# Masking the keys of a decoder's cross attention before they are spread over even and odd heads

## The chip, the cores and the metric

The kernel runs on one core of one Trainium2 chip. Its time is the device time of one launch in microseconds (us), and less is better. Times of several launches are given as a median with the lowest and the highest.

## What is computed

Sixteen independent samples of 128 tokens and 256 features pass through a two-layer decoder in float32. Layer 0 has a causal attention over 16 heads with rotary positions, a linear cross attention and a gated feed-forward part whose operands are rounded to a 4-bit grid. Layer 1 has a causal attention with two score products, a softmax cross attention with a feed-forward part of 1024 hidden features, and a last product whose operands are rounded to a 6-bit grid. A layer normalisation stands after each of the six parts. The change lies in the softmax cross attention of layer 1, of which this is the core:

```python
Q = _split_heads(x @ Wq + bq)          # 16 heads of 16
K = _split_heads(y @ Wk + bk)
V = _split_heads(y @ Wv + bv)
scores = jnp.einsum('bhqd,bhkd->bhqk', Q, K) * scale
scores = jnp.where(mask == 0, jnp.float32(-1000000000.0), scores)
probs = jax.nn.softmax(scores, axis=-1)
attn = jnp.einsum('bhqk,bhkd->bhqd', probs, V)
```

`y` is the context and `mask` has one whole number for each of the 128 context tokens. The kernel sets a masked key to zero (it multiplies the keys by `mb`, which is 0 or 1) and adds the large negative number in the score product through a further small matmul with `mr`.

## The kernel before

**Work of one sample.** The function `stages(b, s)` runs sample `b` in place `s`, one of `NS = 8` sets of buffers, through `l0_attn`, `l0_xattn`, `l0_ffn`, `l1_attn`, `l1_xattn` and `l1_ffn`. Each of these is a generator. Between two `yield`s stands a step: the instructions of mostly one engine. A `yield` names the engine of the next step and what this needs: tiles that must be written, and places in shared rings such as `"p"` (four PSUM banks for products), `"quad"` (the single score tile of four banks) or `"t2"`.

**The order of the work.** All engines stand under a manual schedule: each executes its instructions in the order in which they were recorded. The loop at the end of `decoder_kernel` writes this order when the program is built. It keeps a `Clock` with modelled costs of every instruction (`Timed._cost`), asks each live sample when its next step could begin (`Run.start`), and takes among the steps that could begin within 0.05 of the earliest one by a rank of readiness, age and a table `DELAY`. So the order depends on the modelled cost of each step, and one other cost or one further step can change the order of all later steps of all samples. The DMA issues of SyncE (context, mask, input, output) are recorded in the same order.

**Fillers.** Where the plan leaves TensorE idle for 1.4 us or more, `Timed.fill` records matmuls without use (`ps_filler`, line 161) for three quarters of the planned gap, at a price of 512 columns each. They keep TensorE active.

**The cross attention's keys.** `l1_xattn` (line 1106) loads the mask (`mi`), makes `mb` and `mr` on VectorE, and projects the context into the PSUM tile `ps_x1k`: 2 x 128 columns, two groups of dense features. The score product needs a head on 32 partitions of which half are zero, so `by_parity` (line 560) writes four groups of 128 columns to `k`, two with the even heads and two with the odd heads, by four ScalarE activations that multiply by a column of zeros and ones (`parity`) and add a bias that has been multiplied by the same column (columns 14 to 17 of `bc`). GpSimd then multiplies the 512 columns of `k` by `mb`, in place. The query tile `q` takes a buffer of the ring `B` of its place at the start of the function, and is written only after the query product.

**Names of the later steps.** In `l1_attn` the last product is `ps_op_a` (`out_proj`), with `ps_yt` ahead of it. In `l1_xattn` follow `ps_x1k`, `ps_x1v` (values), `ps_tr_x` (transposition of the sample's state, copied to `yT_x`), `ps_x1q` (query product), `ps_s_x` (scores, whose maxima `nm_x` VectorE takes), `ps_tm_x` (transposed maxima), `ps_st_x` (transposed scores, to `e_x` by the exponential), `ps_yp_x` (weighted values, copied to `ys_x`), `ps_ty_x`, `ps_tr_x1y`, `ps_op_x` (output product), `ps_tr_x1t`, and the feed-forward part: two halves of the first product and the second product, all called `ps_ff` in the profile. In `l1_ffn` VectorE rounds the state (`f1q`, with one step `fc_f` on ScalarE), and `ps_tr_f`, `ps_op_f` and the last layer normalisation lead to `out`.

Of the kernel before, what the change touches and what calls it, by code (L numbers as in the profile page):

```python
# [11 lines left out]
AF = mybir.ActivationFunctionType  # L12
ALU = mybir.AluOpType
AX = mybir.AxisListType

B, T, D, H, HD, LAT = 16, 128, 256, 16, 16, 32
P = 128
# [196 lines left out]
def decoder_kernel(ctx: ExitStack, tc: tile.TileContext, a: dict, out: bass.AP):  # L214
    nc = tc.nc
    clock = Clock()
    V, S, PE, GP = (
        Timed(clock, n, e) for n, e in (("V", nc.vector), ("S", nc.scalar), ("PE", nc.tensor), ("GP", nc.gpsimd))
    )
# [12 lines left out]
    def ring(pool, tag, bufs, shape, dtype, name):  # L232

        t = pool.tile(shape, dtype, tag=tag, name=name, bufs=bufs)
        held = rings.setdefault(tag, [])
        size[tag] = bufs
        opened.append(t)
        clock.kept.add(clock.key(t))
        if len(held) >= bufs:
            old = min(held, key=clock.ends)  # L240
            held.remove(old)
            clock.read[Clock.key(t)] = ("", clock.done(old))
        held.append(t)
        return t

    def mine(s, tag, shape, name, dtype=F32):

        return ring(own, f"{tag}{s}", 1, shape, dtype, name)
# [34 lines left out]
    def arrives(t):  # L283
        clock.wrote[clock.key(t)] = ("Q", max(clock.free["PE"], clock.free["Q"]) + 2.5)
# [53 lines left out]
    def row(name):  # L338
        at = ROW[name]
        return rows[:, at.start - NADD : at.stop - NADD]  # L340
# [55 lines left out]
    parity, parity_half = (const.tile([P, 2], F32, tag=n, name=n) for n in ("parity", "parity_half"))  # L396
# [41 lines left out]
    def bank(shape, name, dtype=F32):  # L438
        return psum(ps_p, "p", shape, name, dtype)

    def work(tag, bufs, shape, name, dtype=F32):
        return ring(wk, tag, bufs, shape, dtype, name)
# [29 lines left out]
    def bias_row(p, name):  # L472

        if name == "l2o":
            g, src = 0, bl
        else:
            g, c, n = place[name]
            src = bt[:, c : c + n]
        PE.matmul(p, lhsT=sel[:, g, :], rhs=src, start=True, stop=False)
# [15 lines left out]
    def layernorm(dst, h, name):  # L495
        m, r, mr = yield from moments(h, name)
        GP.tensor_scalar(mr, m, r, -1.0, ALU.mult, ALU.mult)
        yield "S", mr, h
        S.activation(dst, h, AF.Identity, bias=mr, scale=r)

    def layernorm_affine(dst, h, g, shift, name):

        m, r, _ = yield from moments(h, name)
        yield "V", m
        V.scalar_tensor_tensor(h, h, m, row(g), ALU.subtract, ALU.mult)
        yield "V", r, shift, h
        V.scalar_tensor_tensor(dst, h, r, shift, ALU.mult, ALU.add)
# [3 lines left out]
    def new_x(b, s, name):  # L511

        return mine(s, "x", [P, D], f"x_{name}_{b}")
# [10 lines left out]
    def project(p, weight, rhs):  # L524

        for c in range(p.shape[1]):
            for kc in range(2):
                PE.matmul(
                    p[:, c, :], lhsT=weight[:, kc, c * P : (c + 1) * P], rhs=rhs[:, kc, :], start=(kc == 0),
                    stop=(kc == 1),  # L530
                )

    def biased(dst, p, bias, func=AF.Identity, scale=1.0):

        for c in range(p.shape[1]):
            S.activation(dst[:, c, :], p[:, c, :], func, bias=bias[:, c : c + 1], scale=scale)

    def dense_col(name):
        at = 2 * [n for n, _, _ in DENSE].index(name)
        return bc[:, at : at + 2]  # L540

    def product(p, lhsT, weight, name):

        bias_row(p, name)
        n = lhsT.shape[1]
        for c in range(n):
            PE.matmul(p, lhsT=lhsT[:, c, :], rhs=weight[:, c, :], start=False, stop=(c == n - 1))
# [12 lines left out]
    def by_parity(dst, p, at):  # L560

        for o in range(2):
            biased(dst[:, 2 * o : 2 * o + 2, :], p, bc[:, at + 2 * o : at + 2 * o + 2], scale=parity[:, o : o + 1])
# [108 lines left out]
    def with_bias(b, s, name, tag):  # L672

        t = mine(s, tag, [P, D], f"xb_{name}_{b}")
        GP.tensor_tensor(t, xs[b], row(name), ALU.add)
        return t

    def features(y, s, at, name):

        yT = mine(s, at, [P, 2, P], f"yT_{name}")  # L680
        yield from transposed(y, 2, yT, name)
        return yT

    def out_proj(yT, weight, bias, residual, s, at, name):

        yield "PE", "p", yT
        p = bank((D,), f"op_{name}")
        product(p, yT, weight, bias)
        yield "V", p
        h = mine(s, at, [P, D], f"h_{name}")  # L690
        V.tensor_tensor(h, p, residual, ALU.add)
        return h
# [124 lines left out]
    def values(s, name):  # L817

        v = mine(s, "v", [P, H * VW + HD], f"v_{name}")
        GP.memset(v[:, H * VW :], 0.0)  # L820
        return v
# [284 lines left out]
    def l1_xattn(b, s, ctx_):  # L1106
        yield "V", "mi"
        mi = work("mi", 2, [P, P], f"mi_{b}", I32)
        nc.sync.dma_start(out=mi, in_=a["mask"][:, b * T : (b + 1) * T].partition_broadcast(P))
        q = mine(s, "B", [P, 2, P], f"x1q_{b}")  # L1110
        k = mine(s, "C", [P, 4, P], f"x1k_{b}")
        arrives(mi)
        yield "V", "mb", mi

        mb = work("mb", 2, [P, P], f"mb_{b}")
        V.tensor_scalar(mb, mi, 0.0, None, ALU.not_equal)
        mr = mine(s, "mr", [P, P], f"mr_{b}", BF16)
        V.tensor_scalar(mr, mi, 0.0, terms, ALU.is_equal, ALU.mult)
        yield "PE", "p", ctx_, mb
        p = bank((2, P), f"x1k_{b}")  # L1120
        project(p, w["w_x1k"], ctx_)
        yield "S", p, mb
        by_parity(k, p, 14)
        yield "GP", k, mb
        GP.tensor_tensor(k, k, mb.unsqueeze(1).to_broadcast([P, 4, P]), ALU.mult)
        yield "PE", "p", ctx_
        p = bank((H * VW,), f"x1v_{b}")
        product(p, ctx_, w["w_x1v"], "x1v")
        yield "S", p
        v = values(s, f"x1_{b}")  # L1130
        S.copy(v[:, : H * VW], p)
        xT = yield from features(xs[b], s, "A", f"x1_{b}")
        yield "PE", "p", xT
        p = bank((2, P), f"x1q_{b}")
        project(p, w["w_x1q"], xT)
        yield "S", p
        biased(q, p, dense_col("x1q"), scale=HD**-0.5)
        y = yield from attention(b, s, q, k, v, mr, f"x1_{b}", "A")
        yT = yield from features(y, s, "B", f"x1y_{b}")
        h = yield from out_proj(yT, w["w_x1o"], "x1o", xs[b], s, "D", f"x1_{b}")  # L1140
        t = mine(s, "C", [P, D], f"x1_{b}")
        yield from layernorm_affine(t, h, "g1", row("be1"), f"x1i_{b}")
        tT = yield from features(t, s, "B", f"x1t_{b}")
        ff = []
        for i in range(2):
            yield "PE", "p", tT
            p = bank((4, P), f"ff_{b}_{i}")
            project(p, w["w_1"][:, :, 4 * i * P : 4 * (i + 1) * P], tT)
            yield "S", p
            ff.append(mine(s, "AD"[i], [P, 4, P], f"ff{i}_{b}"))  # L1150
            biased(ff[i], p, cols[:, COL["b1"].start + 4 * i : COL["b1"].start + 4 * i + 4], AF.Relu)
        xb = with_bias(b, s, "be2", "B")
        yield "PE", "p", ff[0]
        p = bank((D,), f"ff2_{b}")
        bias_row(p, "x1b2")
        for c in range(8):
            if c == 4:
                yield "PE", ff[1], p
            PE.matmul(p, lhsT=ff[c // 4][:, c % 4, :], rhs=w["w_2"][:, c, :], start=False, stop=(c == 7))
        yield "V", p  # L1160
        h = mine(s, "A", [P, D], f"h_ff_{b}")
        V.tensor_tensor(h, p, t, ALU.add)
        z = mine(s, "C", [P, D], f"z_x1_{b}")
        yield from layernorm_affine(z, h, "g2", xb, f"x1j_{b}")
        xs[b] = new_x(b, s, "x1")
        yield from layernorm(xs[b], z, f"x1_{b}")
# [14 lines left out]
    def stages(b, s):  # L1181
        ctx_ = yield from l0_attn(b, s)
        yield from l0_xattn(b, s, ctx_)
        yield from l0_ffn(b, s)
        ctx_ = yield from l1_attn(b, s)
        yield from l1_xattn(b, s, ctx_)
        yield from l1_ffn(b, s)
        release(f"place{s}", [xs[b]])
# [214 lines left out]
```

## Time and profile before

| what | value |
|---|---|
| device time, median of three | 964.27 us (961.06 to 965.34) |
| device time of the profiled execution | 960.91 us |
| its span, first to last instruction | 959.2 us |
| TensorE matmuls busy | 891.0 us (93%) |
| TensorE weight loads busy | 711.3 us (74%) |
| VectorE busy | 701.0 us (73%) |
| ScalarE busy | 515.7 us (54%) |
| GpSimd busy | 432.5 us (45%) |
| DMA, mean | 27 GB/s |

The profile comes from one execution, whose own time is 1.71 us above its span and 3.36 us below the median. Busy times of different engines lie beside each other, so they don't add up. In the groups of instructions each row has an engine, an operation, the tile written and those read, the count, then the summed busy time and the mean in ns, and behind the second bar the idle time of the engine ahead of these instructions and what ended it. Nearly all rows have line 208, that of the recording helper, so they are told apart by tiles. Sample numbers are left out of tile names in the profile; they stand in the recorded order of the built program.

### The profile page before, as it was taken

The page shows a single profiled execution, that of the slowest core. Times are in us where ns is not written, and L with a number is a line of the kernel's source. Part 1 is how long each engine was busy: PE and PEld are TensorE (multiplying, and loading weights), DVE is VectorE, ACT ScalarE, POOL GpSimd, SP SyncE. Part 2 cuts the span into 40 slices and gives each one's busy share as a digit, 9 for nine tenths or more (in the row PEclk, how much of TensorE's full clock was granted, in tenths as well). Part 3 has the DMA queues.
Part 4 walks back from the last instruction along what each step waited for, and adds up shares of the span by engine and source line. Part 5 has one row for each costly group of instructions (what it writes and reads, how often), then busy time and mean ns, then how long its engine had stood idle before and what let it go on. Part 6 is the DMA issues. An engine that isn't in the chain of part 4 may idle for free.

```text
span 959.2 us, 28184 instructions
## 1 busy us (share of the span) xinstructions
PE 891.0 (93%) x11882; PEld 711.3 (74%) x11882; DVE 701.0 (73%) x1440; ACT 515.7 (54%) x1119; POOL 432.5 (45%) x898
## 2 busy tenths in 40 slices
PE   6788999899999999999999999998999999999985
PEld 6575666676878788878887776776777878877863
DVE  5899999778975945554768788759858687654564
ACT  3254374475577555555455456546765664654532
POOL 3325444465444446343444454554435353453332
PEclk9999999999999999999999999999999999999998
DMA  7920100000000000010000000000000000100000
GB/s 232 207 71 7 29 13 2 15 10 10 11 23 5 12 27 20 18 30 13 13 15 27 23 25 23 13 13 11 15 10 7 16 6 2 37 5 24 2 12 11
DMA packets 47863, 25.55 MB, mean 27 GB/s; under 512 B 23005, under 2 KB 45517, under 8 KB 47481
## 3 DMA queue, kind: packets, MB, share of 16 engines
q1 hardware_dynamic: 46816, 22.39, 8.6%
q8 instruction: 93, 1.52, 0.6%
q0 software_dynamic: 192, 0.93, 0.4%
q10 hardware_dynamic: 728, 0.44, 0.2%
q14 instruction: 34, 0.27, 0.1%
HBM read 19.57 MB, written 2.10 MB: 23 GB/s over the span
## 4 chain that ended last, share of the span: by engine, by line
PE 53%; DVE 30%; ACT 6%; POOL 6%; issue 4%; POOLq 0%; ACTq 0%; DVEq 0%
PE ps_ff L208 10%; PE ps_s_a L208 3%; DVE nm_a L208 3%; PE ps_st_a L208 3%; DVE rope L208 3%; PE ps_a1qk L208 2%; DVE hh L208 2%; PE ps_st_x L208 2%; PE ps_qk L208 2%; PE ps_dn L208 2%; PE ps_pg L208 2%; PE ps_yt L208 2%; PE ps_pu L208 2%; PE ps_yp_a L208 2%; PE ps_s_x L208 2%
## 5 line engine op out<-in xcount | busy, mean ns | idle before, releaser
L208 POOL TENSOR_SCALAR_AFFINE_SELECT e_a<-e_a 128x1024 f32<-128x1024 f32 x64 | 78.4, 1227 | 75.4 <-ACT e_a L208 75.2
L208 DVE TENSOR_REDUCE nm_a<-ps_s_a 128x16 f32<-128x2048 f32 x32 | 73.1, 2283 | 17.3 <-PE ps_s_a L208 17.2
L208 ACT ACTIVATE e_a<-ps_st_a 128x1024 f32<-128x1024 f32 x64 | 65.7, 1032 | 17.7 <-PE ps_st_a L208 17.5
L208 ACT ACT_TABLE_LOAD x47 | 60.3, 1283 | 12.7 <-DMA brow<-in_rows_dram 8.8
L208 PE MATMUL ps_ff<-yT_x1t,w 128*128 128x128 f32 x512 | 62.9, 276 | 0.5 <-ACT yT_x1t L208 0.5
L208 PEld LDWEIGHTS ps_ff<-yT_x1t,w 128*128 128x128 f32 x512 | 60.1, 192 | 2.4 <-issue 0.9
L208 PE MATMUL ps_ff<-w,ff 128*128 128x256 f32 x256 | 61.3, 383 | 0.0
L208 PEld LDWEIGHTS ps_ff<-w,ff 128*128 128x128 f32 x256 | 46.3, 190 | 7.6 <-issue 1.8
L208 ACT ACTIVATE ff<-ps_ff,cols 128x128 f32<-128x128 f32 x128 | 36.6, 370 | 27.4 <-PE ps_ff L208 27.0
L208 POOL CAST maxima<-nm_a 128x16 bf16<-128x16 f32 x32 | 9.8, 307 | 89.1 <-DVE nm_a L208 89.1
L208 PE MATMUL ps_dn<-qw_down,hT 128*128 128x256 f32 x192 | 47.5, 384 | 1.1 <-ACT yT_x1t L208 1.1
L208 DVE TENSOR_REDUCE nm_x<-ps_s_x 128x16 f32<-128x2048 f32 x16 | 36.5, 2282 | 11.4 <-PE ps_s_x L208 11.4
L208 PE MATMUL ps_pg<-gu,yT_xq 128*128 128x352 f32 x128 | 44.1, 467 | 0.1
L208 PE MATMUL ps_pu<-gu,yT_xq 128*128 128x352 f32 x128 | 43.1, 459 | 0.0
L208 ACT ACTIVATE x_x<-z_x,rstd_x 128x256 f32<-128x256 f32 x32 | 19.2, 601 | 42.5 <-POOL rstd_x L208 39.2
L208 PEld LDWEIGHTS ps_dn<-qw_down,hT 128*128 128x128 f32 x192 | 34.6, 190 | 8.0 <-issue 2.1
L208 ACT ACTIVATE e_x<-ps_st_x 128x1024 f32<-128x1024 f32 x32 | 31.5, 1023 | 15.7 <-PE ps_st_x L208 15.7
L208 ACT ACTIVATE x_a<-h_a,rstd_a 128x256 f32<-128x256 f32 x32 | 19.3, 603 | 31.8 <-POOL rstd_a L208 30.6
L208 PE MATMUL ps_yp_a<-e_a,v_a 128*32 128x128 f32 x1024 | 35.3, 276 | 1.1 <-POOL e_a L208 1.1
L208 POOL TENSOR_TENSOR rot<-rope,rope 128x512 f32<-128x512 f32 x16 | 21.3, 1330 | 29.6 <-DVE rope L208 27.8
L208 PEld LDWEIGHTS ps_pu<-gu,yT_xq 128*128 128x128 f32 x128 | 24.3, 190 | 13.5
L208 POOL TENSOR_TENSOR x1k<-x1k,mb 128x512 f32<-128x512 f32 x16 | 21.8, 1365 | 27.2 <-ACT x1k L208 27.2
(367 smaller groups left out, 2638.0 us busy)
## 6 DMA issues: line engine op xcount, KB each, us to landing
ctx<-in_ctxT_dram SPq DMA_DIRECT2D x32, 128.0 KB
xT_in<-in_xT_dram SPq DMA_DIRECT2D x16, 128.0 KB
w<-in_w_dram SPq DMA_DIRECT2D x2, 1024.0 KB
x_in<-in_x_dram SPq DMA_DIRECT2D x16, 128.0 KB
out_dram<-out SPq DMA_DIRECT2D x16, 128.0 KB
a1qa<-x_f SPq DMA_DIRECT2D x16, 127.0 KB
mi<-in_mask_dram SPq DMA_DIRECT2D x16, 64.0 KB
rows<-in_rows_dram POOLq DMA_DIRECT2D x1, 768.0 KB, 5.7
```

Of the source, the lines that this page charges most:

```text
L208: return f(*args, **kw)
```

## The change

The projection is no longer spread and then masked. Two activations write the dense keys with their bias to a new tile `kb` of 2 x 128 columns, GpSimd multiplies these 256 columns by `mb` in place, and two further activations of 256 columns each write them to `k`, multiplied by the column of even heads and by that of odd heads. A step of ScalarE after GpSimd's is new. `kb` lives in the ring `B`, so `q` is taken from this ring later, just ahead of its writing.

```diff
         mi = work("mi", 2, [P, P], f"mi_{b}", I32)
         nc.sync.dma_start(out=mi, in_=a["mask"][:, b * T : (b + 1) * T].partition_broadcast(P))
-        q = mine(s, "B", [P, 2, P], f"x1q_{b}")
         k = mine(s, "C", [P, 4, P], f"x1k_{b}")
...
         p = bank((2, P), f"x1k_{b}")
         project(p, w["w_x1k"], ctx_)
         yield "S", p, mb
-        by_parity(k, p, 14)
-        yield "GP", k, mb
-        GP.tensor_tensor(k, k, mb.unsqueeze(1).to_broadcast([P, 4, P]), ALU.mult)
+        kb = mine(s, "B", [P, 2, P], f"x1kb_{b}")
+        biased(kb, p, dense_col("x1k"))
+        yield "GP", kb, mb
+        GP.tensor_tensor(kb, kb, mb.unsqueeze(1).to_broadcast([P, 2, P]), ALU.mult)
+        yield "S", kb
+        for o in range(2):
+            S.activation(k[:, 2 * o : 2 * o + 2, :], kb, AF.Identity, scale=parity[:, o : o + 1])
         yield "PE", "p", ctx_
...
         project(p, w["w_x1q"], xT)
+        q = mine(s, "B", [P, 2, P], f"x1q_{b}")
         yield "S", p
         biased(q, p, dense_col("x1q"), scale=HD**-0.5)
```

`biased` issues one activation for each group of 128 columns. Nothing is changed in the table `DELAY`, in the modelled costs or in any other stage, and columns 14 to 17 of `bc` are still computed.

## Prediction

> **What bounds the kernel now.** I read the page first (busy rows, slices, chain), then the groups by form, then the windows, then the end of the timeline.
>
> ```profile
> PE 891.0 (93%) x11882; PEld 711.3 (74%) x11882; DVE 701.0 (73%) x1440; ACT 515.7 (54%) x1119; POOL 432.5 (45%) x898
> PE   6788999899999999999999999998999999999985
> PE 53%; DVE 30%; ACT 6%; POOL 6%; issue 4%; POOLq 0%; ACTq 0%; DVEq 0%
> ```
>
> TensorE is full from slice 6 to slice 37; the chain of waits lies on it for 53%, on GpSimd for 6%. The slack is at the two ends.
>
> ```profile
> L208 ACT ACTIVATE x1k<-ps_x1k,bc,parity 128x128 f32<-128x128 f32 x64 | 24.1, 461 | 16.1 <-PE ps_x1k L208 16.1
> L208 POOL TENSOR_TENSOR x1k<-x1k,mb 128x512 f32<-128x512 f32 x16 | 21.8, 1365 | 27.2 <-ACT x1k L208 27.2
> L208 ACT ACT_TABLE_LOAD x47 | 60.3, 1283 | 12.7 <-DMA brow<-in_rows_dram 8.8 <-PE ps_st_a L208 2.3 <-PE ps_pg L208 0.8
> L161 PE MATMUL ps_filler<-ones,ident_b 128*128 128x512 bf16 x99 | 23.0, 379 | 0.0
> ```
>
> These are the rows touched, the table loads and the fillers. The masked keys are early: the last sample's mask product ends at 897.2 (895.94 + 1.27), its score matmuls start at 910.24. Over all samples the least distance between these two is 11.3 us (first sample, 247.3 to 258.5). The queries come last, so the keys are on no path.
>
> ```profile
> 244.00:850.00 606.00, 585.39 (x7947) 477.64 (x7946) 430.34 (x872) 350.51 (x763) 282.44 (x596) 1.00 0.06 17
> 885.00:960.00 75.00, 60.04 (x568) 49.01 (x566) 40.44 (x104) 28.27 (x76) 24.02 (x57) 0.96 0.02 8
> ```
>
> Columns: stretch, length, busy PE, PEld, DVE, ACT, POOL, then clock and DMA. In the body TensorE idles 20.6 of 606 us; in the last 75 us no engine is full. There latency counts:
>
> ```profile
> 884.11 1.03 PE L208 MATMUL ps_op_a<-w_a1p,yT_a 128*128 128x256 f32 x4
> 932.76 0.41 PE L208 MATMUL ps_tr_x1t<-ident,x 128*128 128x128 f32 x2 [1.07 <-DVE x L208]
> 943.93 5.34 PE L161 MATMUL ps_filler<-ones,ident_b 128*128 128x512 bf16 x24
> 951.21 0.44 PE L208 MATMUL ps_tr_f<-ident,f1q 128*128 128x128 f32 x2 [1.94 <-DVE f1q L208]
> 955.87 0.60 ACT L208 ACTIVATE out<-h_f,rstd_f 128x256 f32<-128x256 f32 x1 [3.82 <-POOL rstd_f L208]
> ```
>
> The last sample leaves `l1_attn` with `ps_op_a` (its step starts at 884.0), and 75.2 us later the span ends.
>
> **What the Trainium skill says.** "ScalarE: Activation LUTs", section "What ACT_TABLE_LOAD costs": a load takes about 1283 ns, a column operand adds about 93 ns, an element 0.833 ns. The trace agrees: 1283 ns, and 461 ns with two columns against 370 with one. "GPSIMD Engine Reference", section 3.1: about 2.6 cycles of 1.2 GHz per element for a two-input product. The trace has 1365 ns for 512 columns and 763 to 807 for 256 (`xb_be`, `xb_x0b`), so about 2.7. "TensorE: Matmul & The Clock Gate", section "What's actually happening": an idle window of 3.4 us halves the clock. The trace shows it once late: `ps_yt` of four matmuls took 1.23 us at 878.70 and 0.61 at 868.83.
>
> **The change part by part.**
>
> GpSimd: 16 products of 512 become 16 of 256, 16 x (1.365 - 0.785) = 9.3 us less busy. It has 55% free: worth nothing on the path.
>
> ScalarE: before, four activations in 1.51 us. After, two of 128 columns (0.66, as `x1q`) and two of 256 from SBUF with one column: an estimate from the skill's prices, 186 + 93 + 213 = 492 ns, of which neighbours overlap 93, so 0.89 for two. Sum 1.55: 16 x 0.04 = +0.6 us. Its new wait on GpSimd holds what is queued behind the spreading (evacuations, for which TensorE waits). The recorded order puts other work between, so I take nothing; bounds -14 us (16 banks free 0.86 us earlier) to +16 us (16 stalls of 0.8 plus two hops of 0.1). The keys come about as early as before (2.9 us); 11 us of slack cover that.
>
> DMA: SyncE issues the same transfers, but from its 63rd row on in another order (a context ahead of a mask). A transfer behind an output waits for that output; the late ones carry nothing that is needed within some us. I take nothing; 0 to +2 us.
>
> Order: this is what moves the time. TensorE's recorded order is the same up to the first keys (row 1161 of 4583, about 245 us), then another one for good. Counted in the built programs: non-filler matmuls 6978 in both, fillers 99 and 121, table loads 47 and 39, changes of tile shape 340 and 345. Table loads: 8 x 1.283 = 10.3 us of ScalarE, not the bound; at a fifth (TensorE waits for ScalarE among others) 2 us.
>
> *Up to the last `ps_op_a`.* A step's price is the distance from its start to the next where they follow at once: half of the first feed-forward product 1.79, the second 3.57, keys 0.89, `ty` 0.44, a two-piece transposition 0.22, `op_x` 0.97, a filler 0.22. In the new order sample 12's feed-forward product (7.14) and sample 13's `ty`, `tr_x1y` and `op_x` (1.63) stand ahead of sample 15's `ps_op_a`, sample 14's keys (0.89) behind it: +7.9 us. Fillers ahead of it: 75 before, 63 now: -12 x 0.22 = -2.7. It would start at 884.0 + 7.9 - 2.7 = 889.2, at equal losses.
>
> *After it.* Less is left for TensorE (45.0 us by these prices, not 52.9), but it is of samples 14 and 15 almost alone, which now go in lockstep: 13 is nearly done, where before 12 to 15 followed each other at distances. Fillers there: 58, not 24. Chained from the rows, from the start of `ps_op_a`:
> - TensorE runs 14.2 us of steps up to both `tr_x`. `x1q` of 14 is queued on ScalarE behind `x_x` of sample 13, due 6.0 us after the feed-forward product (11.7), so 17.8; with the copies and the score product 19.6. VectorE has sample 13's rounding ahead of the maxima: they end at 22.6.
> - The one score tile then serialises the two samples: scores 15 (1.3), maxima (2.4), transposed scores 14 (1.7), exponentials with two copies between (2.9), transposed scores 15 (1.7), exponentials (2.0): 34.6. TensorE is half idle here. Weighted values 1.1, copy 0.7, `ty` 0.6, division 0.8, transposition and copy 0.9, `op_x` 1.5: 40.2.
> - Normalisation, `tr_x1t`, copy 3.4; then 14.5 of feed-forward steps for two samples: 58.1 (before: 11.3 from `op_x` to its end, alone).
> - From there 18.1 as before (941.1 to 959.2), plus some 3 for sample 14's rounding among it on VectorE: 79.2.
>
> The end: 889.2 + 79 = 968, less 2 for the table loads: 966; two further half-clock windows in the half idle stretch at up to 1.7 us each, half of it counted: 967.7. That is 8.5 above the span of 959.2; with 1.7 to the execution's time and 3.4 to the median, 972.8; I say 972.5.
>
> **The rivals.** 0.5%, 4.8 us, is about what a measurement of this kernel can tell from no change.
> - *Slower by the drain* (as above), 972.5; its own range 969 to 988, the upper end with ScalarE's stalls or another ordering loss of 16 us. For: 58 fillers behind the last `ps_op_a`, the single score tile, the length of the chain. Against: my chain may count waits twice. 0.67.
> - *Faster: the body absorbs it.* The 7.9 us pulled ahead fill TensorE's body idle. By start distances, its losses from 250 to 885 are about 52 us beyond priced steps and fillers. If they fall by over 13 us (972.5 to below 959.5), a quarter, the kernel is faster; at a fall of a third, 17 us, it is 955. For: 12 fewer fillers ahead, 10.3 us less on ScalarE, banks freed 0.86 us earlier. Against: only 20.6 us show as idle, the rest is changes between tiles that stay. 0.18.
> - *Nothing is seen*: half of that, 6.5 us, 966. The edit itself is worth nothing, since no key is waited for. 0.15.
> - *The edit does not halve GpSimd's work*: excluded, the built program has 16 products of 256 columns.
>
> **How the numbers follow.** The likeliest case gives 972.5. The range takes in the faster case at 955 and the slower at 988. Faster by over 0.5% 0.18, within 0.15, slower 0.67.
>
> **What would show it.** GpSimd's key product near 0.79 us, x16; table loads x39, fillers x121; score matmuls still over 10 us after the keys. Right: the last `ps_op_a` starts at 885 to 892, and about 79 us follow, with TensorE half idle between the two score products of the last samples and VectorE's maxima next to ScalarE's exponentials in the chain. Wrong: under 75 us after it, or a start before 880 (the body packs better), or ScalarE waiting long for GpSimd's `x1kb`.

## The result, and the profile after

The changed kernel takes 980.01 us in the median of six launches (974.91 to 981.03), the kernel before 962.63 us (961.06 to 965.34). The ratio is 1.0175, with a 95% interval of 1.0153 to 1.0197: slower by 17 us, where 8 had been forecast. The profiled execution took 980.93 us with a span of 979.2, that of before 960.91 with 959.2. The difference of the spans, 20.0 us, is what the traces can explain.

The page of the kernel after, its busy times, TensorE's slices and the chain of waits by engine:

```profile
PE 905.3 (92%) x11902; PEld 718.1 (73%) x11904; DVE 696.8 (71%) x1440; ACT 502.6 (51%) x1111; POOL 426.7 (44%) x898
...
PE   6888899899999899999999999999999989998896
...
PE 48%; DVE 31%; POOL 8%; ACT 7%; issue 5%; DMA 1%; SPq 0%; ACTq 0%; POOLq 0%; DVEq 0%
```

All other engines have less to do than before, GpSimd 5.8 us and ScalarE 13.1 us less. Only TensorE, with its weight loads, is busy longer, and the slices show holes (an 8 among the 9s) where there were none: 14, 33, 37 and 38. The chain lies on TensorE for 48% instead of 53%. The groups by form, with the rows of the edit, the table loads and the fillers:

```profile
L208 ACT ACTIVATE x1k<-x1kb,parity 128x256 f32<-128x256 f32 x32 | 14.6, 511 | 4.8 <-POOL x1kb L208 4.8
L208 POOL TENSOR_TENSOR x1kb<-x1kb,mb 128x256 f32<-128x256 f32 x16 | 13.3, 832 | 16.1 <-ACT x1kb L208 16.1
...
L208 ACT ACT_TABLE_LOAD x39 | 50.0, 1283 | 12.8 <-DMA brow<-in_rows_dram 9.0 <-PE ps_st_a L208 2.3 <-PE ps_pg L208 0.8
L161 PE MATMUL ps_filler<-ones,ident_b 128*128 128x512 bf16 x121 | 29.0, 388 | 0.0
```

GpSimd's product has shrunk from 21.8 to 13.3 us. ScalarE waits for it 4.8 us in all, and no row of TensorE names the keys. The windows (columns as before):

```profile
244.00:850.00 606.00, 580.17 (x7894) 472.96 (x7898) 420.65 (x860) 335.21 (x747) 272.08 (x581) 0.99 0.06 16
...
898.00:980.00 82.00, 65.69 (x576) 48.17 (x567) 34.31 (x91) 27.18 (x70) 22.03 (x53) 0.94 0.03 11
```

In the same 606 us of the body TensorE does 5.2 us less, and its clock is 0.99 instead of 1.00. The last `ps_op_a` starts at 898.59 us (before: 884.0), and 80.6 us follow (before: 75.2). So 14.6 us come ahead of it and 5.4 behind it. TensorE's waits between 244 and 898 us, with their sum, count and longest:

```profile
PE ps_dn L208 <- DVE y_a L208: 4.0, 1, 4.0
PE ps_tr_x1t L208 <- ACT silu L208: 3.5, 1, 3.5
```

Each is a single wait. In the kernel before no single wait between 244 and 880 us was longer than 2.2 us (the first row of its list, with sum, count and longest):

```profile
PE ps_ty_a L208 <- ACT ys_a L208: 2.7, 2, 2.2
```

From the timeline of TensorE in the kernel after, the end:

```profile
900.07 1.13 PE L208 MATMUL ps_op_a<-w_a1p,yT_a 128*128 128x256 f32 x4 [1.21 <-ACT yT_a L208]
...
917.93 1.20 PE L208 MATMUL ps_s_x<-x1k,x1q 32*128 32x128 f32 x32 [0.74 <-ACT x1q L208]
919.07 2.33 PE L161 MATMUL ps_filler<-ones,ident_b 128*128 128x512 bf16 x10
922.46 0.40 PE L208 MATMUL ps_s_x<-mr,ones 3*128 3x512 bf16 x4 [1.07 <-DVE nm_x L208]
...
930.08 2.97 PE L161 MATMUL ps_filler<-ones,ident_b 128*128 128x512 bf16 x9
...
956.01 3.62 PE L208 MATMUL ps_ff<-w,ff 128*128 128x256 f32 x16
959.46 4.70 PE L161 MATMUL ps_filler<-ones,ident_b 128*128 128x512 bf16 x21
...
971.20 0.41 PE L208 MATMUL ps_tr_f<-ident,f1q 128*128 128x128 f32 x2 [0.52 <-DVE f1q L208]
```

Between the score products of the two last samples TensorE has only fillers, and the second one (922.46) waits for the maxima of the first: the two samples take turns at the one score tile.

### The profile page after: what moved, and what is told of

It reads as the page before. It is cut to its first block, busy times and chain, and to the rows that moved or that the text cites. A ratio compares the mean times of both kernels' runs of the same rounds, so it can differ in the third digit from the quotient of the medians.

```text
span 979.2 us, 28221 instructions
## 1 busy us (share of the span) xinstructions
PE 905.3 (92%) x11902; PEld 718.1 (73%) x11904; DVE 696.8 (71%) x1440; ACT 502.6 (51%) x1111; POOL 426.7 (44%) x898
## 4 chain that ended last, share of the span: by engine, by line
PE 48%; DVE 31%; POOL 8%; ACT 7%; issue 5%; DMA 1%; SPq 0%; ACTq 0%; POOLq 0%; DVEq 0%
PE ps_ff L208 9%; PE ps_dn L208 3%; DVE rope L208 3%; DVE hh L208 3%; PE ps_s_a L208 3%; PE ps_a1qk L208 3%; PE ps_st_x L208 2%; DVE nm_a L208 2%; PE ps_st_a L208 2%; ACT L208 2%; PE ps_pg L208 2%; DVE xq L208 2%; PE ps_pu L208 1%; PE ps_op_a L208 1%; PE ps_s_x L208 1%
## 5 line engine op out<-in xcount | busy, mean ns | idle before, releaser
L208 DVE TENSOR_REDUCE nm_a<-ps_s_a 128x16 f32<-128x2048 f32 x32 | 73.1, 2284 | 17.6 <-PE ps_s_a L208 17.4
L208 ACT ACTIVATE e_x<-ps_st_x 128x1024 f32<-128x1024 f32 x32 | 31.6, 1021 | 21.1 <-PE ps_st_x L208 21.1
L208 DVE SCALAR_TENSOR_TENSOR rope<-ps_lat,cols,cosT 128x512 f32<-128x512 f32 x32 | 23.8, 743 | 19.5 <-PE ps_lat L208 17.7
L208 DVE TENSOR_TENSOR h_ff<-ps_ff,x 128x256 f32<-128x256 f32 x16 | 6.8, 424 | 41.7 <-PE ps_ff L208 41.5
```

The source lines that it names most:

```text
L208: return f(*args, **kw)
```

## The experiments

**The theory and its rivals.** The prediction held that the recorded order makes the time and the edit itself nothing. Its rivals: the edit's new wait makes it; or the order counts only through single waits, which could be taken out; or the end's fillers hold up real work. The runs are compared by the prediction's own sum. "Work" and "fillers" are the steps ahead of the last `ps_op_a` at the prediction's prices, which are estimates from start distances in the trace of before. "Losses" is the rest of the time up to the start of this `ps_op_a`, "behind" the time from there to the end, and "work left" the priced work in that stretch. All are in us and rounded each by itself.

| kernel | work | fillers | losses | start of last `ps_op_a` | behind | work left |
|---|---|---|---|---|---|---|
| before | 772.5 | 16.7 | 94.8 | 884.0 | 75.2 | 52.9 |
| after | 780.4 | 14.0 | 104.2 | 898.6 | 80.6 | 45.0 |
| e0_changed_again | 780.4 | 14.0 | 104.0 | 898.4 | 80.6 | 45.0 |
| e1_edit_old_order | 772.5 | 16.7 | 95.4 | 884.6 | 77.2 | 52.9 |
| e2_old_edit_new_order | 780.4 | 14.0 | 106.0 | 900.4 | 80.9 | 45.0 |
| e3_price_only | 782.5 | 14.7 | 122.7 | 919.9 | 70.1 | 42.9 |
| f1_silu_first | 780.4 | 14.0 | 98.8 | 893.2 | 79.2 | 45.0 |
| f2_two_swaps | 780.4 | 14.0 | 95.4 | 889.8 | 79.2 | 45.0 |
| f3_delay6 | 763.4 | 11.3 | 99.9 | 874.7 | 84.9 | 62.0 |
| f5_old_delays | 756.1 | 12.0 | 86.0 | 854.1 | 90.1 | 69.3 |
| g1_delays_old_edit | 756.1 | 12.0 | 88.2 | 856.3 | 90.8 | 69.3 |
| g2_no_drain_fillers | 780.4 | 14.0 | 102.7 | 897.1 | 84.5 | 45.0 |

Part of the losses is the start-up. Up to the first `ps_x1k` the recorded order is the same in before, after, e0 to e2, f1, f2 and g2, and these executions reach it between 243.0 and 248.0 us.

**e0_changed_again**: the changed kernel once more, beside the next three.

> The changed kernel as it is, a second profile of it. Theory (the recorded order costs the time): ratio near 1.0175 to the kernel before, and the same places lose time again: the last ps_op_a starts near 898 us, about 80 us follow, and TensorE stands about 3.5 us for a silu behind a table load near 791 us. Rival (chance of one execution): the profile's losses lie elsewhere, by over 5 us in the body or after the last ps_op_a.

979.53 us (976.94 to 980.69), ratio 1.0179 [1.0158, 1.0200]. From 90 us on the trace repeats the first to 0.3 us, the wait for `silu` and the stretches of half clock included (half clock: the trace records a granted TensorE clock of 0.50). The losses belong to this order and are no accident of one execution.

**e1_edit_old_order**: the order is planned with the old instructions' costs (`charge` books a cost and issues nothing), and the new instructions are issued (those through `nc` are not booked).

```diff
-        by_parity(k, p, 14)
+        for o in range(2):
+            for c in range(2):
+                at = 14 + 2 * o + c
+                charge(S, "activation", k[:, 2 * o + c, :], p[:, c, :], bc[:, at : at + 1], parity[:, o : o + 1])
+        for c in range(2):
+            nc.scalar.activation(q[:, c, :], p[:, c, :], AF.Identity, bias=dense_col("x1k")[:, c : c + 1])
         yield "GP", k, mb
-        GP.tensor_tensor(k, k, mb.unsqueeze(1).to_broadcast([P, 4, P]), ALU.mult)
+        wide = mb.unsqueeze(1).to_broadcast([P, 4, P])
+        charge(GP, "tensor_tensor", k, k, wide)
+        nc.gpsimd.tensor_tensor(q, q, mb.unsqueeze(1).to_broadcast([P, 2, P]), ALU.mult)
...
         S.copy(v[:, : H * VW], p)
+        for o in range(2):
+            nc.scalar.activation(k[:, 2 * o : 2 * o + 2, :], q, AF.Identity, scale=parity[:, o : o + 1])
```

> The new instructions in the order of the kernel before: the planner is charged for the four activations and the product of 512 columns as before, but the dense keys are written to q's buffer, masked in 256 columns and spread by two activations behind the copy of the values. All other instructions stand as before on every engine. Theory (the order costs the time, the edit nothing): ratio 0.997 to 1.003, span near 959, the last ps_op_a near 884, 75 us after it. Rival (ScalarE's wait for GpSimd and the longer activations cost the time): 1.01 to 1.0175, with waits of ScalarE for x1q's masking in the list of waits.

962.02 us (959.07 to 963.57), ratio 0.9995 [0.9981, 1.0009]. In the old order the edit is worth nothing that can be seen, and 17 us of the slowdown are gone. One part of the edit is not tried here: the spreading stands behind the copy of the values, and ScalarE never stood for GpSimd's product ahead of it. That wait is judged by the next run, which has none of it, and by f3_delay6, which has 4.3 us of it.

**e2_old_edit_new_order** is the mirror image: the order of the changed kernel, the instructions of before.

```diff
-        biased(kb, p, dense_col("x1k"))
+        for c in range(2):
+            charge(S, "activation", kb[:, c, :], p[:, c, :], dense_col("x1k")[:, c : c + 1])
+        for o in range(2):
+            for c in range(2):
+                at = 14 + 2 * o + c
+                nc.scalar.activation(
+                    k[:, 2 * o + c, :], p[:, c, :], AF.Identity, bias=bc[:, at : at + 1], scale=parity[:, o : o + 1]
+                )
         yield "GP", kb, mb
-        GP.tensor_tensor(kb, kb, mb.unsqueeze(1).to_broadcast([P, 2, P]), ALU.mult)
+        charge(GP, "tensor_tensor", kb, kb, mb.unsqueeze(1).to_broadcast([P, 2, P]))
+        nc.gpsimd.tensor_tensor(k, k, mb.unsqueeze(1).to_broadcast([P, 4, P]), ALU.mult)
         yield "S", kb
         for o in range(2):
-            S.activation(k[:, 2 * o : 2 * o + 2, :], kb, AF.Identity, scale=parity[:, o : o + 1])
+            charge(S, "activation", k[:, 2 * o : 2 * o + 2, :], kb, parity[:, o : o + 1])
```

> The instructions of the kernel before in the order of the changed one: the planner is charged for the dense keys, the product of 256 columns and the spreading, but by_parity's four activations and the product of 512 columns are issued. All other instructions stand as in the changed kernel. Theory (order): ratio 1.015 to 1.02 to the kernel before, span near 978, the last ps_op_a near 898, about 80 us after it. Rival (the edit's own instructions): 0.997 to 1.005.

982.15 us (979.88 to 983.03), ratio 1.0206 [1.0186, 1.0226]. The order alone gives the slowdown without one edited instruction. In this order the edit even takes 2.6 us away (e0 against e2), though the two intervals overlap.

**e3_price_only**: the kernel before, with one planned cost changed. GpSimd's product is booked at 256 columns and issued at 512.

```diff
-        GP.tensor_tensor(k, k, mb.unsqueeze(1).to_broadcast([P, 4, P]), ALU.mult)
+        charge(GP, "tensor_tensor", k[:, :2, :], k[:, :2, :], mb.unsqueeze(1).to_broadcast([P, 2, P]))
+        nc.gpsimd.tensor_tensor(k, k, mb.unsqueeze(1).to_broadcast([P, 4, P]), ALU.mult)
```

> The kernel before with one thing changed in the planner: GpSimd's key product is charged as 256 columns while 512 are issued, so all instructions are those of before, in a third order (115 fillers, the last ps_op_a has 42.9 us of TensorE work behind it and 782.5 ahead, as against 52.9 and 772.5). Theory (any other order is likely to lose, most where the last samples are left alone): ratio 1.01 to 1.035, the last ps_op_a later than 892 and 75 us or more behind it. Rival (the order of the changed kernel is singular, a plan's order hardly matters otherwise): 0.995 to 1.005.

990.12 us (988.19 to 991.77), ratio 1.0286 [1.0261, 1.0311]. A booked cost moves the time by 28.6 us. But the place was missed: the stretch behind the last `ps_op_a` is shorter than before (70.1), and the losses ahead of it are 27.9 us higher. Little work at the end does not by itself make an order slow, and losses in the body are not equal between orders.

**f1_silu_first** and **f2_two_swaps** look at the two long single waits of the new order. Around 791 us ScalarE stands like this in the kernel after (its timeline):

```profile
791.37 0.24 ACT L208 COPY mT_x<-ps_tm_x 128x128 bf16<-128x128 bf16 x1
791.64 1.28 ACT L208 ACT_TABLE_LOAD   x1
792.93 1.02 ACT L208 ACTIVATE e_a<-ps_st_a 128x1024 f32<-128x1024 f32 x1
793.97 1.28 ACT L208 ACT_TABLE_LOAD   x1
795.26 0.46 ACT L208 ACTIVATE silu<-ps_pg 128x352 f32<-128x352 f32 x1
```

and TensorE, which waits for that `silu`, runs the next product of `ps_ff` at half clock (granted from 795.3 us, for 6.8 us), 3.78 us where others of its kind show 1.95:

```profile
795.78 0.69 PE L208 MATMUL ps_tr_x1t<-ident,x 128*128 128x128 f32 x2 [3.46 <-ACT silu L208]
796.93 3.78 PE L208 MATMUL ps_ff<-yT_x1t,w 128*128 128x128 f32 x16 [0.46 <-ACT yT_x1t L208]
```

The recording helper is given a table of calls to be held back until another one has been issued. The plan books them where they stood, so the rest of the order stays. For f1:

```diff
+HOLD = {('S', 875): ('S', 876), ('GP', 744): ('S', 876)}
...
             self._c.run(self._n, aps[0], aps[1:], cost, after)
-            return f(*args, **kw)
+            at, self.i = (self._n, self.i), self.i + 1
+            if at in HOLD:
+                HELD.setdefault(HOLD[at], []).append((f, args, kw))
+                return None
+            r = f(*args, **kw)
+            for g, x, y in HELD.pop(at, []):
+                g(*x, **y)
+            return r
```

The numbers count the calls of an engine: `e_a` of sample 13 and GpSimd's mask on it go behind the `silu` of sample 15. f2 puts the two products `hh<-hh,fc_h` behind `ri_a` and `y_a` as well. In the kernel after VectorE runs them first, while TensorE stands 4.03 us for `y_a` (timelines of VectorE and TensorE):

```profile
319.01 3.16 DVE L208 TENSOR_TENSOR hh<-hh,fc_h 128x704 f32<-128x704 f32 x2
322.09 0.25 DVE L208 RECIPROCAL ri_a<-ps_ty_a 128x16 f32<-128x16 f32 x1
322.37 0.42 DVE L208 TENSOR_TENSOR y_a<-ps_ty_a,ri_a 128x256 f32<-128x256 f32 x1
...
322.94 2.49 PE L208 MATMUL ps_dn<-qw_down,hT 128*128 128x256 f32 x8 [4.03 <-DVE y_a L208]
```

The edit of f2 against f1:

```diff
-HOLD = {('S', 875): ('S', 876), ('GP', 744): ('S', 876)}
+HOLD = {('S', 875): ('S', 876), ('GP', 744): ('S', 876), ('V', 525): ('V', 528), ('V', 526): ('V', 528)}
```

> The changed kernel, with one exponential of sample 13 (and GpSimd's mask on it) issued after the second silu of sample 15 instead of before it; all else in the same order. This takes two table loads away, and with them what the 3.46 us stand of TensorE at 791.5 us waits for. Theory A (single waits of the new order are carried to the end): the stand and the 6.8 us at half clock right behind it (3.4 us lost) both go, so the last ps_op_a starts about 7 us earlier, near 891.6, and the time is near 972.5 (970 to 975). Theory B (the order as a whole is slower, and a wait taken away is followed by another): the last ps_op_a stays within 2 us of 898.5 and the time at 977.5 to 980.

> As f1_silu_first, and besides two VectorE products of the first layer's feed-forward part (hh<-hh,fc_h, 3.16 us together) are issued after the two small instructions ri_a and y_a that TensorE waits for at 319 us (4.03 us, followed by a stretch at half clock of 3.4 us, 1.7 us lost). Theory A: a further 4 to 5.7 us, 966 to 969. Theory B: as f1_silu_first within 1.5 us, since 580 us of other work follow in which 4 us can be absorbed.

f1: 975.67 us (974.05 to 979.15), ratio 1.0159 [1.0119, 1.0198]. f2: 972.69 us (970.70 to 973.35), ratio 1.0119 [1.0086, 1.0153]. The time of f1 lies between the two theories (970 to 975 for A, 977.5 to 980 for B). To leave out the start-up I set the traces against e0 at equal amounts of work done. f1 is 2.9 us ahead of e0 from 90 us on, stays so within 0.1 us for 700 us, and at 791 us the 2.8 become 5.3: the swap is worth 2.5 us there, not 7. TensorE in f1 (line numbers are shifted by the edit) shows why:

```profile
789.76 0.41 PE L215 MATMUL ps_tr_x1t<-ident,x 128*128 128x128 f32 x2 [0.26 <-DVE x L215]
792.30 3.68 PE L215 MATMUL ps_ff<-yT_x1t,w 128*128 128x128 f32 x16 [2.14 <-ACT yT_x1t L215]
```

The transposition goes at once, but the copy behind it is now what comes after the remaining table load: a wait of 2.14 us takes the place of the 3.46, and one stretch of half clock remains. For the second swap theory A holds in the trace: it had 4 to 5.7 us. (The medians of f1 and f2 differ by 3.0; the 966 to 969 us forecast for f2 were missed, since the first swap brought less.) The wait of 4.03 us for `y_a` falls to 0.84 in TensorE's timeline:

```profile
317.82 1.97 PE L215 MATMUL ps_dn<-qw_down,hT 128*128 128x256 f32 x8 [0.84 <-DVE y_a L215]
```

f2's lead over e0 grows there from 1.9 to 6.3 us, by 4.4 (the stretch of half clock behind the wait, 3.4 us long, is gone too), and is still 6.0 when the `silu` comes 460 us later. Hardly anything of it is absorbed.

**f3_delay6** changes one entry of the table by which the order is chosen, in the changed kernel:

```diff
-DELAY = (0.04, 0.26, 0.15, 0.27, 0.15, 0.52, 0.34, 0.45, 0.56, 0.30, 0.28, 0.08, 0.47, 0.04, 0.22, 0.10, 0.51)
+DELAY = (0.04, 0.26, 0.15, 0.27, 0.15, 0.52, 0.51, 0.45, 0.56, 0.30, 0.28, 0.08, 0.47, 0.04, 0.22, 0.10, 0.51)
```

> The changed kernel with one entry of the table DELAY changed, sample 6's from 0.34 to 0.51: the same instructions but for fillers (81, not 121; 39 table loads as in the changed kernel), in a fourth order, with 62 us of TensorE's priced work behind the last ps_op_a instead of 45. If the order alone makes the time, this moves it by many us although nothing is edited in the cross attention: 763.4 us of work and 11.3 of fillers ahead, with losses between those of the kernel before (94.8) and of the changed one (104.2), put the last ps_op_a at 869 to 879, and 62 us of work plus about 22 of latency behind it the time at 955 to 965. If the price is in the changed cross attention itself, it stays at 977 to 982.

959.57 us (957.41 to 962.51), ratio 0.9987 [0.9971, 1.0003]. One number in the table takes the whole slowdown back, with the edit in place. The start of the last `ps_op_a` (874.7), the losses (99.9) and the time fall into the forecast ranges.

**f5_old_delays** is e1_edit_old_order with another table, and **g1_delays_old_edit** is the kernel before with that table and nothing else.

```diff
+DELAY = (0.22, 0.52, 0.27, 0.57, 0.24, 0.44, 0.39, 0.15, 0.17, 0.3, 0.31, 0.48, 0.4, 0.27, 0.54, 0.21, 0.44)
```

> The new instructions issued in an order that is planned with the old ones' costs (as in e1_edit_old_order), with another table DELAY throughout: 78 fillers and 33 table loads, 756.1 us of priced work and 12.0 of fillers ahead of the last ps_op_a, 69.3 behind it. By the same sum, with losses of 95 to 104, the last ps_op_a starts at 863 to 872, and 69.3 + about 20 behind it give 952 to 961, so faster than both kernels if losses don't grow. If the losses go with the order as they did in e3_price_only (122.7), about 980.

> The kernel before with the table DELAY of f5_old_delays and nothing else changed: the order of f5_old_delays with the four spread activations and the product of 512 columns. If the order makes the whole gain of f5_old_delays, it is within 3 us of its 946.2, so 943 to 949, with the last ps_op_a near 854 and 90 us behind it. If the 256-column product is what pays there (9 us less of GpSimd, banks free 0.86 us earlier in 16 places), it is slower than 949, up to 958.

f5: 946.22 us (944.32 to 947.36), ratio 0.9846 [0.9806, 0.9885]. g1: 946.51 us (946.46 to 948.81), ratio 0.9844 [0.9825, 0.9863]. Both beat the kernel before and the changed one, by the order alone; the edit makes no difference in this order either. The gain is larger than forecast: the losses are 86.0 us, where I had taken 95 to 104. The page of f5:

```profile
PE 884.2 (94%) x11861; PEld 709.2 (75%) x11861; DVE 700.6 (74%) x1440; ACT 494.2 (52%) x1105; POOL 427.5 (45%) x898
...
PE   6788789999999999999999999999999999999995
...
PE 56%; DVE 29%; POOL 6%; ACT 5%; issue 4%; POOLq 0%; DVEq 0%; ACTq 0%
```

TensorE is at nine tenths or more from slice 7 to slice 39, and the 90.1 us behind the last `ps_op_a` hold 69.3 us of work.

**g2_no_drain_fillers**: the changed kernel, in which the 58 fillers behind the last `ps_op_a` are booked and not issued (`DRAIN` is set when sample 15 comes to this product).

```diff
-            self._e.matmul(bank, lhsT=lhsT, rhs=rhs, start=True, stop=True)
+            if not DRAIN:
+                self._e.matmul(bank, lhsT=lhsT, rhs=rhs, start=True, stop=True)
```

> The changed kernel in its own order, with the 58 fillers behind the last ps_op_a not issued (the 63 ahead of it stay). It tells what the half-idle end is made of. Theory A (waits along the chain of samples 14 and 15 set the end, and fillers lie in gaps): still 78 to 82 us behind the last ps_op_a; a clock halved more often may add up to 4 us, so 978 to 984. Theory B (the fillers, 12.9 us of them, hold up steps that are ready): 70 to 77 us behind it and 970 to 977.

984.49 us (981.62 to 986.87), ratio 1.0235 [1.0203, 1.0267]. Behind the last `ps_op_a` it takes 84.5 us, 3.9 more than with the fillers. Its page, TensorE's slices and the granted clock:

```profile
PE   6788999899999999999999999999999989999783
...
PEclk9999999999999899999999999999999989999796
```

Without fillers two stretches at half clock, 17.1 us from 920.1 and 19.1 us from 964.5, cover over half of the last 62 us; with them these are 6.8 and 5.1 us. The rival, 70 to 77 us behind the last `ps_op_a`, is out: taken together the fillers hold nothing up. They pay 3.9 us in the traces and 5 in the medians, where up to 4 were expected, so both values lie a little above their ranges (78 to 82 and 978 to 984).

## Why the prediction was right, and where its size was off

**Right: the edit is worth nothing on the path, the order moves the time.** The estimates held: 0.728 us in the median (0.832 in the mean, since some products took up to 1.364) for the 256 columns against 0.785 estimated, 0.89 to 0.91 us for two spreading activations against 0.89. ScalarE's new wait came to 4.8 us in five places and reached TensorE in none. e1 and e2 together show both halves: 0.9995 for the edit without the order, 1.0206 for the order without the edit. "Nothing" holds to a few us. From the first keys to the last `ps_op_a` the single traces put the edit 4.4 us ahead in the old order (e1 against before), 4.3 ahead in the new one (e0 against e2) and 1.3 behind in that of f5 (against g1); the medians show none of it in the first and third order and 2.6 us in the second. In the first two pairs a stretch of 3.4 us at half clock less is part of this. One gain can be named. In the kernel before TensorE stands 1.16 us at 291.4 us for the spreading of the keys (`ps_tr_x1t` waits for ScalarE's `x1k`); in e1 the like wait, for the two dense activations, is 0.3. So the words that the keys are on no path were not quite right. The score matmuls start at least 8.4 us after their keys, a little less than the 10 I had named.

**Right: the end.** I had 79.2 us after the last `ps_op_a`, and up to 1.7 for half-clock windows; it is 80.6, and f1 and f2, whose orders differ from the changed one only at one and two earlier places, have 79.2. Both score products, the maxima and the exponentials stand in the chain as predicted. Two rows of it:

```profile
920.21 2.21 DVE nm_x L208
934.71 1.95 ACT e_x L208 x2
```

Counted from the start of `ps_op_a`, the first score product ends at 20.5 us (19.6 in my chain), the exponentials at 38.1 (34.6), the feed-forward part at 60.9 (58.1), and 19.7 us follow (21.1). Most of the excess is clock: in the changed kernel a stretch of half clock, 6.8 us from 925.0, falls on the transposed scores. f1 and f2 have none there, and show 35.6, 58.4 and 20.8 us: each within 1.0 us of the chain. What the two lockstepped samples cost is seen in the table: behind minus work left is 35.6 us in the changed kernel, 34.2 in f1 and f2, and 20.8 to 27.2 in the four other orders. That the single score tile makes most of this is argued from the timeline and was not tried by itself; g2 excludes the fillers.

**Off: "It would start at 884.0 + 7.9 - 2.7 = 889.2, at equal losses".** It started at 898.6, so the sign named for being right, 885 to 892, was missed. The 7.9 and the 2.7 are counted in the program and stand; the losses were not equal, they rose by 9.4 us (94.8 to 104.2). Of this 3.0 came before the two orders part, where executions of the same instructions differ by up to 5 us. The other 6.4 are in the body, and they are a balance. By order alone the losses of the body grow by 10.6 us from before to e2 and by 10.7 from e1 to e0, and the edit takes the 4.3 to 4.4 back. f1 and f2 price two waits at 2.5 and 4.4 us, half clock included: 6.9 of the 10.6. The rest was not followed. So most of it was not many small changes between tiles. Twice a queue had long work of another sample ahead of a short instruction that TensorE needed: an exponential with two table loads ahead of a `silu` on ScalarE, and 3.16 us of `hh` ahead of `y_a` on VectorE. Both stand in the recorded order and could have been looked for there.

**Off: "less 2 for the table loads".** Eight table loads went, 10.3 us of ScalarE, and no gain from it is seen. The count was the wrong measure. In f1 two loads fewer bring 2.5 us, because TensorE stood behind them; with eight fewer, spread over the program, the losses rose. Loads were not tried apart from their places.

**The sum again**, in spans: work +7.9, fillers -2.7, losses of the start-up +3.0, of the body +6.4, the end +5.4, together 20.0. The median differs by 17.4, because both profiled executions lie on different sides: that of before 1.7 below its median of six launches, that of after 0.9 above.

**The rival "the body absorbs it"** needed losses falling by over 13 us; they rose. In f5 they do fall, by 8.8, so it was a fair rival, if too large a one.

**What was luck.** The sign of the forecast hung on "at equal losses", for which the prediction had only the ground that most losses are changes between tiles. Against the 94.8 us of the kernel before, the losses of the other orders are 8.8 us lower (f5) to 27.9 higher (e3), so this one term scatters by more than the forecast of 8 us (start-up makes up to 5 of the scatter). The measured time lies in the stated range because this was wide: it reached up to 988, for ScalarE's stalls or "another ordering loss of 16 us", without saying where this would arise. It was an ordering loss; ScalarE's stalls are out, since e2 has none and is as slow.

## What to carry to other kernels

Where a program writes the order of instructions from modelled costs, an edit that changes a cost or adds a step is two changes, and the second can be larger than the first by far: run the edit in the old order and the old code in the new order before judging either. Compare the two orders for a short instruction that frees a buffer of the busiest engine and stands behind a long one of other work; one such wait of 4 us was still felt here 460 us later, almost undiminished. And the table that ranks the steps is a knob of its own: here it was worth 1.5%.

## What was not expected of the hardware

The Trainium skill, "TensorE: Matmul & The Clock Gate", section "What's actually happening", puts the half clock after an idle window of 3.4 us. In these traces the window need not be idle. Ahead of the half-clock stretch at 792.35 us in f1_silu_first TensorE's matmuls were busy for 1.02 of the last 3.41 us (as long as the shortest stretch of half clock in these traces) and its longest stand was 2.14 us; ahead of that at 878.67 us in the kernel before, they were busy for 2.05 us, with no stand longer than 1.14 us in the 12 us before. This second one is the halving that the prediction had taken for an idle window; nor is it the only late one, since the trace of before has others at 656.8 and 953.8 us. Here the measurement decides: a stand of some 2 us can be enough to double the time of the next product (3.68 us for 16 matmuls of `ps_ff` instead of 1.95).

The start is not steady: the same instructions reach the first keys at 243.0 to 248.0 us, and most of the difference arises in the first 90 us; its cause was not looked for. Behind it the lead of one execution over another of the same order can stay the same to 0.1 us for over 500 us (the changed kernel and e0). It is not always so: at some 320 us g2_no_drain_fillers loses 0.9 us to e0 with the same instructions, where its half clock lasts 6.8 us instead of 3.4.
